# Nested 2x2 products for LSTM steps over two and three nodes, with the weight sums made in the graph stage and kept in DRAM

## The chip, the cores and the metric

The kernel runs on one core of one Trainium2 chip. Its time is the device time of one execution, in microseconds, and the median of several runs is given. The profile is of one such execution, taken by the hardware profiler.

## The reference, cut to what matters

Four layers work on `x` of 128 graphs, 64 nodes each, 256 features. The first layer, which holds all that changes, is a pre-norm residual block around two graph convolutions and four LSTMs:

```python
h = relu(layernorm(x))
h = relu(einsum('ts,bsh->bth', adj, h @ Wg0 + bg0))
h = relu(einsum('ts,bsh->bth', adj, h @ Wg1 + bg1))
for p in range(1, 5):                      # windows of p nodes
    nw = 64 // p
    wins = h[:, :nw * p].reshape(128 * nw, p, 256)
    last = lstm_last(Wih[p-1], Whh[p-1], bih[p-1], bhh[p-1], wins)   # p steps, state from zero
    h = h.at[:, arange(nw) * p + p - 1].set(last)
x = x + h

def step(h, c, x_t):                       # gates of 256 each, order i, f, g, o
    i, f, g, o = split(x_t @ Wih.T + h @ Whh.T + bih + bhh)
    c = sigmoid(f) * c + sigmoid(i) * tanh(g)
    h = sigmoid(o) * tanh(c)
```

Everything is float32. Three more layers follow (a batch-normalised graph network, a graph convolution with three weight matrices, an attention); the change does not touch them.

## The kernel before

All activations of the first layer lie feature-major in SBUF: `hT[g]`, four tiles of 128 partitions x 2 feature halves x 2048 tokens. Every engine's instructions are issued in an order that is written out by hand: functions are put on a list as events with a planned time (`at(t, fn, ...)`), the list is sorted, and the functions run in that order. Nothing is reordered afterwards; each engine and the DMA queue of SP work through their instructions in this order and wait where data or a buffer is not there.

**Graph stage** (`graph_part`, 16 rounds of 512 tokens, planned at 10 units a round). SP loads x (`load`, three buffers `xt`), DVE makes the layer norm's statistics (L375, L376, L380), POOL the root (L381), DVE the shift (L384), ACT normalises (L388). TensorE applies the adjacency (L396), the first weights (L406) and the second weights (L435); ACT copies products from PSUM (L400), DVE adds biases (L412, L442, L449). The second weights are applied in a 2x2 product form with seven products instead of eight, for which POOL makes four differences of the data a round (`sums`, L427: the tile `t`). In one of the rounds POOL also makes the four weight sums of the one-node LSTM (`weight_sum`, L313).

**The seven-product form.** A product of a 2x2 block matrix of weights with a 2x2 block matrix of data takes seven block products when four sums of weight blocks (S1 to S4) and four sums of data blocks are at hand. For one gate of an LSTM the weight blocks are the halves of its 256 inputs and 256 outputs, and the data blocks are the two feature halves of two blocks of windows (up to 512 columns each). `gate` issues these products: L701 for the input part and, in steps after the first, L707 for the state part, into the same three PSUM banks `a`, `b`, `c`. DVE and ACT take the banks to a gate tile (L723 adds, L726 copies), ACT applies the sigmoid or tanh (L719), POOL or DVE makes the new cell (L755), ACT its tanh (L760), DVE the new state (L670, L675). `input_sums` (L662) makes the four data differences of the input on DVE into `tx`, `state_sums` (L682 to L685) those of the state. There are five gate tiles and eight banks.

A first step has three gates (the state is zero, f is not needed): 21 products of 512 columns. A later step of the one-level form has four gates, each with seven input and seven state products: 56.

**The nested form** (`outer_step`), used before only for later steps over four nodes. The outer level is again a 2x2 seven-product form: the weight blocks are (input, state) x (gates i and g, gates o and f), the data blocks are x and h of the two window blocks. Of its seven products four (numbers 5, 2, 4, 3: `strassen`, L940) are themselves done in seven half-width products for each of two gates, and three (1, 6, 7: `direct`, L965) in eight plain ones. That is 28 products, each as two halves of 256 columns, and 24 whole ones: 52. The outer data sums are T1 to T4 (L1017, L1020, L1027, L1030), each of the four inner products has four inner data sums (`inner_sum`, L925), and DVE and ACT take the banks (`take`, L952 and L954; `chained`, L974 to L979). The weight sums it needs (S1 to S4 of the outer level and the inner sums of each) are made by POOL in the four-node stage itself (`outer_sum`, L874 to L885; `outer_wih_sum`, L841), and the sums for the one-level form of two and three nodes in the stage before or in their own (`weight_sums`, L313).

Two pairs of window blocks are worked on in turn (A and B), so that one's state is finished on the other engines while TensorE does the other. Two nodes have 4 pairs of 512 columns, three nodes 4 pairs (two of 320 columns and two of 352), four nodes 2 pairs of 512; one node has 8 pairs and only first steps.

Of the kernel before, what the change touches and what calls it, by code (L numbers as in the profile page):

```python
# [14 lines left out]
P = 128  # L15
# [5 lines left out]
def kernel(ctx: ExitStack, tc: tile.TileContext, a: dict, out: bass.AP):  # L21
# [317 lines left out]

    ready = []  # L340
# [12 lines left out]
    with tc.tile_pool(name="pa", bufs=2) as pa, tc.tile_pool(name="pax", bufs=3) as pax:  # L353
# [189 lines left out]
        for s in range(NS):  # L543
            graph_part(s)
        for _, _, fn, args in sorted(events, key=lambda e: e[:2]):
            fn(*args)
# [87 lines left out]
    PLACES = ("c", "a0", "b", "k0", "k1", "a1", "k2", "k3")  # L634
    new_banks(**{n: 1 for n in PLACES})
    turn_ = {"bank": 6, "gate": 0, "a": 0}

    def next_bank():
        turn_["bank"] += 1
        return bank(("c", "a0", "k0", "k1", "a1", "b", "k2", "k3")[(turn_["bank"] - 1) % 8])  # L640

    def gate_tile(k):
        return lg.tile([P, 2, KC, 512], F32, tag=f"gate{k}", name="gate")

    tx = lg.tile([P, 4, 512], F32, tag="tx", name="tx")
    lh1 = lstm.enter_context(tc.tile_pool(name="lh1", bufs=1, reuse_waits="tile"))
    even_state = ExitStack()
    lh0 = even_state.enter_context(tc.tile_pool(name="lh0", bufs=1, reuse_waits="tile"))
    events = []
# [3 lines left out]

    def input_sums(st, j):

        b = [[cols(blk, c, st["p"], j) for c in range(KC)] for blk in st["blk"]]
        t = st["tx"] = [wide(ready[0][:, n, :]) for n in range(2)] if ready else []
        ready.clear()
        yield from t
        for k in range(len(t), 4):  # L660
            t.append(wide(tx[:, k, : st["N"]]))
            yield nc.vector.tensor_sub(t[k], *((b[1][0], b[0][0]), (b[1][1], t[0]),  # L662
                                               (b[1][1], b[1][0]), (b[0][1], t[1 % len(t)]))[k])

    def state(st, n, h_of_o, last, j):

        o, tanh_c = (r["G"] for r in h_of_o)
        if last:
            for c in range(KC):
                nc.vector.tensor_mul(cols(st["blk"][n], c, st["p"], j),  # L670
                                     wide(o[:, n, c, : st["N"]]), wide(tanh_c[:, n, c, : st["N"]]))
            return
        if n == 0:
            st["h"] = st["pool"].tile([P, 2, KC, 512], F32, tag="h", name="h")
        nc.vector.tensor_mul(st["h"][:, n, :, : st["N"]], o[:, n, :, : st["N"]],  # L675
                             tanh_c[:, n, :, : st["N"]])

    def state_sums(st, engine):
        N = st["N"]
        t = st["th"] = (lh0 if st["pool"] is lh0 else sums_of).tile([P, 3, 512], F32, tag="th", name="th")  # L680
        h = st["h"][:, :, :, :N]
        yield engine.tensor_sub(t[:, 0, :N], h[:, 1, 0], h[:, 0, 0])  # L682
        yield engine.tensor_sub(t[:, 1, :N], h[:, 1, 1], t[:, 0, :N])
        yield engine.tensor_sub(h[:, 1, 0], h[:, 1, 1], h[:, 1, 0])
        yield engine.tensor_sub(t[:, 2, :N], h[:, 0, 1], t[:, 1, :N])  # L685

    def gate(t0, st, j, l, w, gi, fn):

        N = st["N"]
        blk, r = st["blk"], {"tag": turn_["gate"] % 5}  # L690
        turn_["gate"] += 1
        wih, whh = w

        def product(bank_, k):
            if bank_ not in r:
                r[bank_] = next_bank()
            first_ = (bank_, k) in (("a", 1), ("b", 5), ("c", 2))
            p_, tx = r[bank_], st["tx"]
            x_ = (cols(blk[0], 0, st["p"], j), cols(blk[0], 1, st["p"], j),
                  cols(blk[1], 1, st["p"], j), *(tx[i] if i < len(tx) else None for i in (3, 0, 1, 2)))[k - 1]  # L700
            nc.tensor.matmul(wide(p_[:, :N]), wih_of(l, k, gi), x_,  # L701
                             start=first_, stop=(j == 0), skip_group_check=True)
            if j:
                h, th = st["h"], st["th"]
                h_ = (h[:, 0, 0, :N], h[:, 0, 1, :N], h[:, 1, 1, :N], th[:, 2, :N], th[:, 0, :N],
                      th[:, 1, :N], h[:, 1, 0, :N])[k - 1]
                nc.tensor.matmul(p_[:, :N], whh[0][:, OF[k], gi, :], h_,  # L707
                                 start=False, stop=True, skip_group_check=True)

        def slot(n, hc):  # L710
            return r["G"][:, n, hc, :N]

        def new():
            r["G"] = gate_tile(r["tag"])

        def act(n, hc, bank_=None):
            m = gi * KC + hc
            to = r["G"][:, :, hc, :N] if n is None else slot(n, hc)
# [9 lines left out]
        at(t0 - 0.01, new)  # L728
# [14 lines left out]
    def wih_of(l, k, gi):  # L743
        w = wt[l][0][0]
        if l < NL - 1:
            return w[:, OF[k], gi, :]
        g, m = ORDER.index(gi), OF[k]
        if m < 4 and k != 7:
            return outer["wx"][:, m, g, :]
        return outer["wxs"][:, (S1, S2, S3, S4).index(m), g, :]  # L750

    def both(fn, st, *tiles):

        def one(n):
            fn(*((t["G"] if isinstance(t, dict) and "G" in t else st["c"])[:, n, :, : st["N"]]  # L755
                 for t in tiles))
        return one

    def tanh_of(o_, c):
        nc.scalar.activation(o_, c, AF.Tanh)  # L760

    def step(t0, st, j, last, l, w, short_next):
        p = st["p"]
        u = 1 / 1.72 if j else 1 / 0.86
        sums = input_sums(st, j)
        for k in (-0.7, 0.1, 6.3, 7.1):
            at(t0 + k, next, sums)
        g, end, t = {}, {}, t0
# [1162 lines left out]
```

## Time and profile before

| | us |
|---|---|
| median of three runs | 1864.84 (1864.15 to 1866.7) |
| the profiled execution | 1864.71 |
| its span, first to last instruction | 1863.0 |
| granted TensorE clock, mean | 0.997 |
| graph stage | 0 to 172 |
| LSTM over one node | 172 to 316 |
| over two nodes | 316 to 582 |
| over three nodes | 582 to 887 |
| over four nodes | 887 to 1206 |
| the other three layers | 1206 to 1863 |

A row of the windows gives, for a stretch of the span: its length, then for each engine its busy time with the number of instructions (PE is the matmuls, PEld the weight loads that overlap them), the granted clock, the mean share of the DMA engines and GB/s. A row of a timeline gives start, length, engine, line, operation, the tiles written and read, the shape, the count of merged instructions, and in brackets the idle time before it with what ended it. One float32 product of the program is two matmul records. Matmuls overlap in the pipeline, so the cost of one in a stream is the distance of starts and not its own length.

### The profile page before, as it was taken

Reading aid. Unit: us, or ns where it says so; the run is one execution under the profiler, and the core shown is the slowest. Engines: PE = TensorE matmul, PEld = TensorE weight load, DVE = VectorE, ACT = ScalarE, POOL = GpSimd, SP = SyncE. Lnnn points to the kernel's source line nnn. Section 1 sums busy time; section 2 is a strip of 40 time slices with the busy share of each in tenths; the row PEclk is TensorE's granted clock in tenths of the full one; section 3 lists DMA queues with packets and bytes.
Section 4 is the critical chain, followed back from the end, with each engine's and each line's share of the span. In section 5 each row is a group of like instructions: output and inputs, shape, how many; then the busy total and the mean of one; then the engine's idle time right before and its main releaser. Section 6 shows DMA issues by size and latency. Waiting matters only on the chain.

```text
span 1863.0 us, 22263 instructions
## 1 busy us (share of the span) xinstructions
PE 1832.1 (98%) x7956; PEld 1234.1 (66%) x7956; DVE 1162.3 (62%) x2250; ACT 964.1 (52%) x1680; POOL 949.1 (51%) x895
## 2 busy tenths in 40 slices
PE   8999999999999999999999999989999999999999
PEld 7997444444445666666466666656544899999997
DVE  6775777634546434444766666688876666666664
ACT  6776666534535334533534444577675454444442
POOL 4441423443423523422787776767454566666663
PEclk9999999999999999999999999999999999999999
DMA  4110000000001000000000000333110101111111
GB/s 136 57 58 0 0 1 23 23 1 0 1 0 46 1 0 1 1 1 1 23 1 1 1 1 0 102 124 114 54 40 1 46 13 46 46 46 46 46 47 35
DMA packets 51694, 55.01 MB, mean 30 GB/s; under 512 B 3456, under 2 KB 46976, under 8 KB 51584
## 3 DMA queue, kind: packets, MB, share of 16 engines
q1 hardware_dynamic: 51136, 53.30, 9.0%
q8 instruction: 63, 1.03, 0.2%
q14 instruction: 47, 0.39, 0.1%
q10 hardware_dynamic: 448, 0.30, 0.1%
HBM read 36.55 MB, written 17.04 MB: 29 GB/s over the span
## 4 chain that ended last, share of the span: by engine, by line
PE 92%; POOL 2%; DVE 2%; ACT 2%; issue 1%; DMA 1%; SPq 0%; POOLq 0%; DVEq 0%; ACTq 0%
PE ps L701 26%; PE ps L707 12%; PE ps L1655 8%; PE ps L940 7%; PE ps L965 6%; PE ps L1265 5%; PE ps L1382 4%; PE ps L396 3%; PE ps L406 3%; PE ps L1742 3%; PE ps L1622 2%; PE ps L435 2%; PE ps L1718 2%; PE ps L1752 2%; PE ps L1783 1%; PE ps L626 1%
## 5 line engine op out<-in xcount | busy, mean ns | idle before, releaser
L723 DVE TENSOR_TENSOR gate<-gate,ps 128x512 f32<-128x512 f32 (+2 forms) x306 | 176.6, 604 | 303.1 <-PE ps L707 227.6
L701 PE MATMUL ps<-tx,wih 128*128 128x512 f32 (+2 forms) x804 | 344.2, 530 | 4.2 <-ACT gate L726 3.3
L701 PE MATMUL ps<-hT,wih 128*128 128x512 f32 (+2 forms) x612 | 265.9, 530 | 0.0
L701 PEld LDWEIGHTS ps<-tx,wih 128*128 128x128 f32 x804 | 152.4, 190 | 148.0 <-issue 96.9
L726 ACT COPY gate<-ps 128x512 f32<-128x512 f32 (+2 forms) x204 | 106.2, 521 | 250.3 <-PE ps L707 195.9
L719 ACT ACTIVATE gate<-gate,lbias 128x512 f32<-128x512 f32 (+2 forms) x204 | 171.7, 842 | 117.1 <-DVE gate L723 117.0
L701 PEld LDWEIGHTS ps<-hT,wih 128*128 128x128 f32 x612 | 116.6, 190 | 108.2 <-issue 70.4
L707 PE MATMUL ps<-h,whh 128*128 128x512 f32 (+2 forms) x384 | 158.6, 494 | 0.0
L755 POOL TENSOR_TENSOR cell<-gate 128x1024 f32<-128x1024 f32 (+2 forms) x34 | 74.8, 2220 | 159.2 <-ACT gate L719 159.2
L755 POOL TENSOR_TENSOR gate<-gate 128x1024 f32<-128x1024 f32 (+2 forms) x24 | 43.9, 1851 | 181.8 <-ACT gate L719 181.8
L954 DVE TENSOR_TENSOR gate<-gate,ps 128x512 f32<-128x512 f32 x120 | 82.0, 683 | 69.4 <-PE ps L940 67.0
L707 PE MATMUL ps<-th,whh 128*128 128x512 f32 (+2 forms) x288 | 118.9, 494 | 0.0
L1598 ACT ACTIVATE h<-x,ln_rn 128x256 f32<-128x256 f32 x128 | 68.0, 592 | 92.8 <-POOL ln_rn L1595 92.7
L1655 PE MATMUL ps<-wl,ag 128*128 128x128 f32 x900 | 108.3, 276 | 0.6
L707 PEld LDWEIGHTS ps<-h,whh 128*128 128x128 f32 x384 | 73.0, 190 | 54.3 <-issue 30.6
L1655 PEld LDWEIGHTS ps<-wl,ag 128*128 128x128 f32 x900 | 104.2, 192 | 3.3 <-ACT ag L1627 2.5
L985 ACT ACTIVATE gate<-gate,lbias 128x512 f32<-128x512 f32 x96 | 64.9, 717 | 57.4 <-DVE gate L954 30.3
L707 PEld LDWEIGHTS ps<-th,whh 128*128 128x128 f32 x288 | 54.7, 190 | 40.7 <-issue 23.0
L755 POOL TENSOR_TENSOR cell<-gate,cell 128x640 f32<-128x640 f32 (+2 forms) x20 | 37.2, 1874 | 67.4 <-ACT gate L719 67.4
L726 DVE COPY gate<-ps 128x512 f32<-128x512 f32 (+2 forms) x102 | 62.0, 608 | 13.0 <-PE ps L707 12.6
L1742 PE MATMUL ps<-wvo,h3T 128*128 128x256 f32 x256 | 65.5, 379 | 0.0
L760 ACT ACTIVATE gate<-cell 128x1024 f32<-128x1024 f32 (+2 forms) x60 | 55.5, 931 | 18.6 <-POOL cell L755 18.6
(317 smaller groups left out, 4098.5 us busy)
## 6 DMA issues: line engine op xcount, KB each, us to landing
xt<-in_x_dram SPq DMA_DIRECT2D x30, 512.0 KB, 3.9
x1d<-xt SPq DMA_DIRECT2D x16, 512.0 KB, 2.9
x<-x1d SPq DMA_DIRECT2D x16, 512.0 KB, 4.8
out_dram<-x SPq DMA_DIRECT2D x15, 512.0 KB, 3.0
wih<-in_WihT_dram SPq DMA_DIRECT2D x12, 256.0 KB, 4.9
whh<-in_WhhT_dram SPq DMA_DIRECT2D x8, 256.0 KB, 5.6
xt<-in_x_dram SPq DMA_DIRECT2D x6, 128.0 KB, 3.5
wl<-in_W_dram SPq DMA_DIRECT2D x4, 192.0 KB, 3.1
```

What stands on the lines that cost most here:

```text
L701: nc.tensor.matmul(wide(p_[:, :N]), wih_of(l, k, gi), x_, start=first_, stop=(j == 0), skip_group_check=True)
L707: nc.tensor.matmul(p_[:, :N], whh[0][:, OF[k], gi, :], h_, start=False, stop=True, skip_group_check=True)
L719: nc.scalar.activation(to, r[bank_][:, :N] if bank_ else to, fn, bias=lbias[:, l, m : m + 1])
L723: nc.vector.tensor_add(slot(n, hc), slot(n, hc), r[bank_][:, :N])
L726: op(slot(n, hc), r[bank_][:, :N])
L755: fn(*((t["G"] if isinstance(t, dict) and "G" in t else st["c"])[:, n, :, : st["N"]] for t in tiles))
L940: nc.tensor.matmul(B[pr, name][:, g * H : (g + 1) * H], w[:, g, :], d, start=(g == 0 and (name, k) in (("a", 1), ("b", 5), ("c", 2))), sto ...
L954: nc.vector.tensor_add(half(pr, hc, d), half(pr, hc, d), v)
L965: nc.tensor.matmul(to, w, d, start=(pr == 1 and c == 0), stop=(c == 1), skip_group_check=True)
L1265: nc.tensor.matmul(r[name], con["w1"][:, OF[j], g, :], x_, start=new, stop=(name, j) in (("a", 4), ("b", 3), ("c", 2)), skip_group_check=True)
L1655: nc.tensor.matmul(v["g", name][:, p_, :], x_[:, m, ts(p_, P)], wl2[:, OF[j], m, :], start=new and p_ == m == 0, stop=m == 2 and (name, j) ...
L1742: nc.tensor.matmul(v["H"][:, q % 2, :], v["h3T"][:, c, ts(q, P)], wvo[:, c, :], start=(c == 0), stop=(c == KC - 1))
```

## The change

All steps after the first, over two and three nodes too, use `outer_step`; `gate` keeps the first steps only, and the one-level later step goes. The weight sums of the LSTMs over two, three and four nodes are made by POOL during the graph stage (`staging`), one layer after the other in one place (`wb`, `wc`), and stored to DRAM (`summed`). The LSTM stages fetch them into places that are free at the time (`places`, `fetch`, `load_r`, `fetch_s3`); for two nodes two places overlap and are refilled in every group. The differences of the input for first steps are made by POOL instead of DVE. The order of banks and gate tiles at group starts is written out, and the inner data sums of the state are planned later in `outer_step`, because three of the inner products share one place for them. The ends of the stage (`begin` and what follows it) keep their planned times in a new unit.

```diff
+    def staging(p):
+        R = wbf[:, :2048].rearrange("p (b g m) -> p b g m", b=4, m=P)
...
+        IG, OF_ = R[:, :, 0:2], R[:, :, 2:4]
+        add, sub = nc.gpsimd.tensor_add, nc.gpsimd.tensor_sub
+        work = [*(inner(W1, k) for k in (0, 1, 3)), *(inner(W2, k) for k in (0, 1, 3)),
+                *(outer(add, S1_, OF_, W2, b) for b in (0, 2)), *(outer(sub, S2_, S1_, IG, b) for b in (0, 2)),
+                inner(W2, 2), *(inner(S1_, k) for k in range(4)),
+                *(outer(sub, S4_, W1, S2_, b) for b in (0, 2)), inner(W1, 2),
+                *(x_sum(k) for k in range(4)), *(inner(S4_, k) for k in range(4)),
+                *(outer(sub, OF_, IG, OF_, b) for b in (0, 2))]
+        stores = {9: ("S2", wbf[:, 5632:6656]), 10: ("W2", w2), 14: ("S1", wcf), 17: ("W1", w1),
+                  21: ("X", wbf[:, 5632:]), 25: ("S4", w2)}
+        loads = [lambda: load("WhhT", W1, ((0, 0), (1, 2))), lambda: load("WhhT", W2, ((0, 3), (1, 1))),
+                 lambda: load("WihT", R, tuple(enumerate(ORDER)))]
+        def last():
+            nc.sync.dma_start(summed[p, "S3"].rearrange("p (b g m) -> p b g m", b=4, m=P), OF_)
...
+        def stage(n, fn):
+            r, k = divmod(n, 6)
+            events.append((30 + ROUND * r + (-0.7, 0.5, 1.7, 2.9, 4.1, 5.3)[k], len(events), fn, ()))
+        for i, p in enumerate(range(2, NL + 1)):
+            work, stores, loads = staging(p)
+            for n, fn in enumerate(work):
+                stage(28 * i + n, fn)
+            for n, fn in stores.items():
+                stage(28 * i + n + 1, fn)
+            for n, fn, t in zip((18, 26, 28), loads, (10.5, 17.5, 24.5)):
+                if i:
+                    stage(28 * (i - 1) + n + 1, fn)
+                else:
+                    events.append((t, len(events), fn, ()))
...
-            yield nc.vector.tensor_sub(t[k], *((b[1][0], b[0][0]), (b[1][1], t[0]),
+            yield nc.gpsimd.tensor_sub(t[k], *((b[1][0], b[0][0]), (b[1][1], t[0]),
...
+    def fetch(p, name, lo=0, hi=7):
+        to = pl[p][name]
+        g = to.parts[0].shape[2]
+        v = summed[p, name].rearrange("p (b g m) -> p b g m", g=g, m=P)
+        hi = min(hi, v.shape[1])
+        cuts = sorted({lo, hi, *(c for c in to.cuts if lo < c < hi)})
+        for b0, b1 in zip(cuts, cuts[1:]):
+            nc.sync.dma_start(to.span(b0, b1), v[:, b0:b1])
...
-        for k in (-0.7, 0.1, 6.3, 7.1):
-            at(t0 + k, next, sums)
+        for k in (-9, -8.5, 0.2, 0.4) if st["new"] else (*((-0.8, -0.6) if p == NL else (-3.4, -1.4)), 2.6, 6.6):
+            at(t0 + k, next, input_)
...
         for c in range(KC):
-            prep(-38 + 0.6 * c, T1, c, needs_h=False)
+            tick((-26 if one else -38) + 0.6 * c, T1, c)
...
-        for k, s in ((0, -25), (1, -24), (3, -23)):
+        prep(-11, T2)
+        prep(-10.9, inner_sum, 5, 2)
+        for k, s in ((0, 1), (1, 2), (3, 3)):
             prep(s, inner_sum, 2, k)
...
-        for k in range(4):
-            prep(late + 2 + k, inner_sum, 4, k)
+        for k, s in ((0, 25), (1, 26), (3, 27), (2, 28)):
+            prep(s, inner_sum, 4, k)
+        for k, s in ((0, 38), (1, 38.5), (3, 39), (2, 39.5)):
+            prep(s, inner_sum, 3, k)
...
+    plan(t, 2, (2, load_r), *((8 + 3 * k, fetch, name) for k, name in enumerate(("X", "W1", "W2", "S1", "S2"))),
+         (25, fetch, "S4", 2, 7), (28, fetch_s3, 0))
     for p in range(1, NL + 1):
...
+            if p == 2:
+                plan(t, p, (8, fetch, "S4", 0, 2))
+            if p == NL:
+                plan(t, p, (8, fetch, "S4"), (8.5, fetch_s3, 0))
+            now = {"22": tags[1], "11": tags[2], "12": tags[3], "21": tags[4], "spare": tags[0]}
+            t += 1
+            for j in range(1, p):
+                for st in sts:
+                    fin = p == NL and j == p - 1 and st is sts[-1]
+                    u = t
+                    t = outer_step(t, st, j, now, fin)
+                    tags = [now[n] for n in ("spare", "11", "21", "12", "22")]
+                    now = dict(now)
+                    now["22"], now["spare"] = now["spare"], now["22"]
+            if p == 2 and not end:
+                plan(u, p, (43, fetch, "X", 2, 4))
+            if end and p < NL:
+                q = p + 1
+                plan(u, q, (12.5, load_r), (36, fetch, "X"), (25.5, fetch, "W1"), (38.5, fetch, "W2"),
+                     (52.5, fetch, "S1"), (53.5, fetch, "S2"))
+                if q < NL:
+                    plan(u, q, (68, fetch, "S4"), (70, fetch_s3, 0))
```

## The prediction

> **What bounds the kernel now.** I read the page's first part, then the windows by stage, then the PE timeline at one place of each stage, then POOL's timeline in the graph stage.
>
> ```profile
> PE 1832.1 (98%) x7956; PEld 1234.1 (66%) x7956; DVE 1162.3 (62%) x2250; ACT 964.1 (52%) x1680; POOL 949.1 (51%) x895
> ```
>
> TensorE is busy 98% of the span, so only fewer matmul columns or fewer stalls can move the time. The stages (busy us: PE, PEld, DVE, ACT, POOL):
>
> ```profile
> 0.00:172.00 172.00, 165.09 (x991) 149.89 (x992) 114.67 (x317) 116.76 (x192) 68.97 (x105) 1.00 0.23 68
> 172.00:316.00 144.00, 143.33 (x334) 63.20 (x334) 105.46 (x156) 97.61 (x134) 38.54 (x18) 1.00 0.00 0
> 316.00:582.00 266.00, 265.58 (x622) 117.80 (x621) 132.66 (x173) 115.13 (x157) 102.53 (x54) 1.00 0.03 8
> 582.00:887.00 305.00, 303.53 (x1066) 201.84 (x1065) 149.64 (x280) 134.56 (x245) 109.75 (x77) 1.00 0.03 8
> 887.00:1206.00 319.00, 312.84 (x1090) 204.14 (x1088) 209.51 (x294) 144.49 (x228) 236.93 (x173) 0.99 0.06 19
> ```
>
> They are the graph stage and the LSTMs over one, two, three and four nodes. No engine but PE is near full, except POOL in the last (74%). What a product costs, from the PE timeline of the four-node stage (already nested) and of the three-node stage:
>
> ```profile
> 946.41 1.03 PE L940 MATMUL ps<-mid,whh 128*128 128x256 f32 x4
> 947.27 1.02 PE L965 MATMUL ps<-th,mid 128*128 128x512 f32 x2
> 948.13 1.03 PE L940 MATMUL ps<-h,whh 128*128 128x256 f32 x4
> ```
> ```profile
> 641.45 0.70 PE L707 MATMUL ps<-th,whh 128*128 128x320 f32 x2
> 641.99 0.76 PE L701 MATMUL ps<-hT,wih 128*128 128x352 f32 x2
> 642.58 0.76 PE L707 MATMUL ps<-h,whh 128*128 128x352 f32 x2
> ```
>
> A product is two records. Starts give 0.86 us for 512 columns, 0.86 for its two halves of 256, 0.54 for 320 and 0.59 for 352.
>
> Stalls, from the PE timeline around the start of the four-node stage:
>
> ```profile
> 906.86 1.88 PE L701 MATMUL ps<-hT,wih 128*128 128x512 f32 x4
> 911.00 2.80 PE L701 MATMUL ps<-tx,wih 128*128 128x512 f32 x4 [2.26 <-ACT gate L726]
> 913.60 1.91 PE L701 MATMUL ps<-hT,wih 128*128 128x512 f32 x2
> 915.30 1.06 PE L701 MATMUL ps<-tx,wih 128*128 128x512 f32 x2
> ...
> 936.18 2.07 PE L965 MATMUL ps<-hT,wih 128*128 128x512 f32 x2 [2.54 <-ACT gate L719]
> ```
> ```profile
> 911.00:940.00 29.00, 26.46 (x67) 13.86 (x68) 18.87 (x20) 13.31 (x20) 28.61 (x22) 0.88 0.00 1
> ```
>
> The 2.26 us gap is followed by products at 1.70 us instead of 0.86 (913.60 to 915.30), and the granted clock is 0.88 in that window. By starts the two stalls cost 4.2 and 4.3 us. POOL is busy 28.61 of 29 us there.
>
> **The change part by part.**
>
> *Products.* An LSTM step after the first takes 2 x 28 = 56 products now and 4 x 7 + 3 x 8 = 52 nested, 28 of them as two halves. Two nodes (512 columns): 4 pairs x 1 step x 4 products x 0.86 = 13.8 us less; the halves add 28 x 0.003 a step (4 x 216 ns against 2 x 429), so 13.4. Three nodes: 4 steps at 320 columns, 4 x 4 x 0.54 = 8.6, and 4 at 352, 4 x 4 x 0.59 = 9.4. Halves of 160 and 176 columns are in no row; 128-column matmuls of L1655 start 112 ns apart, 256-column ones 216. A straight line between them gives 138 and 151 ns, half of the full width plus 1.5 ns gives 136 and 149. So 15.1 to 17.0 us. The sum is 28.5 to 30.3; I take **-29.5**.
>
> [...] The rows above decide: the halves cost 0.86 against 0.86, at 128 columns weight loads still keep up with 112 ns, and 160 lies between. I use the rows.
>
> *Weight sums, moved into the graph stage.* Off POOL in the LSTM stages go L313's wih and whh sums of two and three nodes (8 x 1.34 + 8 x 1.44), L841 (3.9) and L874 to L885 (some 27): about 53 us, 27 of them inside the window at 911. Into the graph stage come 84 sums in 14 rounds of six: 48 of 256 columns (0.70 us from start to start), 24 of 512 (1.25), 12 of 384 (1.0), 76 us, or 5.4 a round. A round:
>
> ```profile
> 88.76 0.73 POOL L427 TENSOR_TENSOR t<-g 128x256 f32<-128x256 f32 x1 [4.97 <-ACT g L400]
> ...
> 92.30 1.01 POOL L381 TENSOR_TENSOR ln_rn<-ln_rn,mhalf 128x4 f32<-128x4 f32 x1
> 93.28 5.10 POOL L313 TENSOR_TENSOR wih<-wih 128x512 f32<-128x512 f32 x4
> 98.81 0.73 POOL L427 TENSOR_TENSOR t<-g 128x256 f32<-128x256 f32 x1 [0.43 <-ACT g L400]
> ```
>
> A round is 10.05 us, four differences and the root take 3.8, so 6.25 are free: 5.4 fits. But the round at 93.3 already holds the 5.1 us of the one-node weights; with its own 5.3 the differences end some 4 us late. PE first reads t at 104.65 and today has 5.1 us of slack, so that alone just fits; the root, 4 us late, holds DVE's L384 (due at 104.62, slack 1.3), behind it ACT's relus and g copy (L400 ends at 107.43, PE needs it at 109.49). Cost: 4 - 1.3 - 2.1 = 0.7 us.
>
> *SP's queue.* Moved ahead of the x loads: 48 weight loads (0.65 us each to issue) and 21 stores, each store behind its POOL sum, and a load into the same place behind the store's landing. At the turn from two to three nodes: S4's sum ends at 74.6, its 0.9 MB store lands about 4 us later (estimate from x1d's 2.9 us for 0.5 MB), four loads to 81.2, S3's store, eight loads to 87, and only then the x load that today goes out at 67.6. It lands at 90.5; DVE's statistics want it at 87.5. DVE stands 3 us, with evictions queued behind it; PE has 2.75 us there. But the root is now late by as much and POOL waits in it, just ahead of the overfull round: t is ready at 106.9 against 104.65, PE stands 2.3 us, then some 1 us for root and relus. The later x loads that follow stores and weight loads come out some 3 us late at worst, which those 2.75 us cover.
>
> [...] The row at 911.00 shows half speed after 2.26 us. [...] by the row some 1.6 us more; I use the row. Graph stage: 0.7 without the late x load, 5 with it, 9 if DVE's stands reach PE too. I take **+4**.
>
> *DMAs in the LSTM stages.* 54 fetches, loads and refills, all behind PE's last read of the place and 6 to 40 us ahead of first use; after the x loads nothing else waits in SP's queue. 0, hidden behind PE's steps; a late one would cost its landing, 3 to 6 us.
>
> *Input differences on POOL.* One-node stage: DVE loses four L662 a step (0.68 to 1.1 us), POOL gains four. L682, 512 columns on POOL, takes 1.27 us. POOL has then 5.1 + 2 x 2.4 = 9.9 of 18 us a step. The tightest is the fourth: it follows both cell products and ends 1.2 us ahead of its reader. 0; if POOL runs as in its contended rows (2.7 for 2.4), up to 0.5 a step, 8 steps, 4 us.
>
> *Other engines in nested steps.* At 320 columns: POOL 8 operations of 640 (1.55) and 16 of 160 (0.53, by the line through 455 ns at 128 and 730 at 256), 21 of 28 us; DVE 32 x 0.48 plus six SBUF operations, 21; ACT 12 x 0.42 + 16 x 0.56 + 1.5 = 16. All below PE. At four nodes the same mix runs with no gap.
>
> *Stalls at group starts.* Now, in starts: 0.7 at 458, 0.4 and 0.9 at 589 and 613, 1.5 at 737, 4.2 and 4.3 at the four-node start: 12 us. After, five groups enter the nested form. Their first steps load ACT with 2 x 10 us plus the tail of the step before (7) in 24 us at three nodes, so some queueing stays: I give each group 1.6 us, as at 737, 8 in all. **-4**. Bounds: -11 (none left) to +10.
>
> Sum: -29.5 + 4 - 4 = -29.5. Against the profiled execution of 1864.71 (span 1863.0 and 1.7 around it; the median of the three runs, 1864.84, is 0.1 above): **1835**.
>
> **The rivals.** *R1, the graph stage hardly notices and nested entries are clean*: for it, POOL's free 6.25 against 5.4 and the gapless four-node steps; against, the overfull round. -29.5 - 10 + 1: 1826. *R2, POOL bounds the graph stage*: if its sums run at contended durations (L925 at 1.04 us for 256, L885 at 1.6 for 512), a round has 7.5 against 6.25, 14 x 1.25 = 17 us, with 4 from the x load: 1852. Against it: in this stage L427 and L313 run uncontended. *R3, slower*: entering the nested form costs what it costs today at the only place where it is entered, 8.5 us. Four more groups enter it: +34 - 29.5, and the graph stage's 4: 1873. It decides from 6.4 us an entry ((29.5 - 4) / 4). Against it: at 911 to 940 POOL was full of weight sums that are gone, and DVE stood behind it:
>
> ```profile
> 900.80 2.68 DVE L662 TENSOR_TENSOR tx<-hT,tx 128x512 f32<-128x512 f32 x1
> ```
>
> *R4, the change does not do what it says* is excluded as to products: the program has 52 of them a step.
>
> **How the numbers follow.** My forecast 0.62 (1835, its bounds 1829 to 1843), R1 0.18, R2 0.14, R3 0.06. The range 1825 to 1847 takes in R1, mine and R2's nearer half. About 0.2% (3.7 us) is what a measurement of this kernel can tell from no change. Faster 0.94, same 0.01, slower 0.05.
>
> **What would show it.** Products: 128x160 and 128x176 records some 136 to 151 ns apart; two- and three-node stages of some 253 and 289 us. Graph stage: POOL near 95%, a PE gap near 105, an x wait of DVE near 87.5, the stage longer by 1 to 9 us. Four-node start: no gap above 2 us. Wrong if halves start over 165 ns apart, if DVE or POOL end waits within the nested steps, or if each group start shows gaps above 3 us.

## The result, and the profile after

| | before | after |
|---|---|---|
| median of four runs each, us | 1864.49 (1862.59 to 1866.70) | 1838.02 (1836.51 to 1839.84) |
| ratio | | 0.9858, 95% interval 0.9841 to 0.9875 |
| the profiled execution, its span | 1864.71, 1863.0 | 1838.82, 1837.1 |
| first LSTM product starts at | 171.8 | 178.7 |
| from it to the last nested product of the four-node stage | 1033.1 | 1000.1 |
| from there to the end | 658.0 | 658.3 |

The change is worth 26.5 us. The LSTM stages lose 33.1 us, the graph stage gains 6.9, the rest is as it was. The last three rows are read off TensorE's starts in the two traces, and are used for every run below.

The first part of the page after, to be read against the line of before that the prediction shows:

```profile
PE 1802.4 (98%) x8532; PEld 1299.3 (71%) x8532; DVE 1196.0 (65%) x2346; ACT 990.8 (54%) x1776; POOL 1211.8 (66%) x1207
```

TensorE still bounds the kernel with 98%, on a shorter span. POOL, 949 us before, has 1212: the staged sums and the input differences.

The windows by stage (graph stage to the first LSTM product; to the first nested product; to the first three-node product; to the first four-node product; to the last nested one). The columns are busy us of PE, PEld, DVE, ACT and POOL, then granted clock, DMA share, GB/s; the length of the stretch stands ahead of them:

```profile
0.00:178.70 178.70, 166.69 (x990) 149.60 (x991) 119.83 (x317) 117.15 (x192) 144.09 (x189) 1.00 0.57 188
178.70:357.31 178.61, 177.94 (x415) 78.62 (x414) 97.65 (x156) 119.90 (x167) 96.45 (x63) 1.00 0.09 33
357.31:575.18 217.87, 217.87 (x732) 138.61 (x730) 133.31 (x184) 100.49 (x153) 140.95 (x104) 1.00 0.09 28
575.18:866.12 290.94, 286.65 (x1450) 231.59 (x1449) 195.89 (x369) 150.70 (x308) 212.50 (x217) 1.00 0.07 23
866.12:1178.76 312.64, 310.50 (x1090) 202.98 (x1089) 199.21 (x290) 145.96 (x231) 224.42 (x168) 1.00 0.06 19
```

Most of TensorE's idle time sits in two rows: 12.0 us in the graph stage (6.9 in the shorter window of before) and 4.3 us in the three-node stage; the four-node stage has 2.1 us. The nested two-node steps have none.

The PE timeline within a three-node step of 352 columns, nested now:

```profile
782.42 0.76 PE L985 MATMUL ps<-hT,wc 128*128 128x352 f32 x2
783.01 0.76 PE L961 MATMUL ps<-h,wb 128*128 128x176 f32 x4
783.61 0.76 PE L985 MATMUL ps<-hT,wc 128*128 128x352 f32 x2
784.20 0.76 PE L961 MATMUL ps<-h,wb 128*128 128x176 f32 x4
```

Four half-width records take 0.60 us (783.01 to 783.61), two whole ones 0.59. By the median of all starts a record of 176 columns takes 149 ns, of 160 columns 136, of 256 columns 216; whole ones of 352, 320 and 512 take 296, 269 and 429.

The graph stage, on TensorE, POOL and DVE:

```profile
97.55 0.67 PE L493 MATMUL ps<-t,wg 128*128 128x256 f32 x2 [2.30 <-DVE h L507]
111.57 0.70 PE L493 MATMUL ps<-g,wg 128*128 128x256 f32 x2 [1.86 <-DVE h L500]
143.02 0.70 PE L493 MATMUL ps<-g,wg 128*128 128x256 f32 x2 [0.94 <-DVE h L500]
```
```profile
89.86 2.54 POOL L370 TENSOR_TENSOR wc<-wb 128x512 f32<-128x512 f32 x2 [2.79 <-DMA wb<-in_WihT_dram]
...
109.39 1.02 POOL L439 TENSOR_TENSOR ln_rn<-ln_rn,mhalf 128x4 f32<-128x4 f32 x1
...
137.29 0.73 POOL L313 TENSOR_TENSOR wb<-wb 128x256 f32<-128x256 f32 x1 [3.47 <-issue]
```
```profile
92.03 0.43 DVE L433 BATCH_NORM_STATS2 ln_st<-xt 128x6 f32<-128x256 f32 x1 [4.19 <-DMA xt<-in_x_dram]
110.45 0.68 DVE L442 SCALAR_TENSOR_TENSOR ln_rn<-ln_mv,ln_rn 128x4 f32<-128x4 f32 x1 [2.94 <-POOL ln_rn L439]
```

Three gaps of TensorE, all released by DVE. DVE was late for x (due near 87.8, there at 92.00) and twice for POOL's root: L439 ends at 110.4, and before the third gap DVE stood another 1.68 us for it, at 141.89. POOL itself stood twice for a weight load of the staging: for R at 89.86, and at 137.29, where the profile names no releaser ("issue") but the last load of the four-node W2 (the third W2) had landed at 137.17.

The largest gaps that are left in the LSTM stages, three-node and four-node starts:

```profile
588.74 1.40 PE L853 MATMUL ps<-tx,wih 128*128 128x320 f32 x4 [1.70 <-ACT gate L869]
...
674.36 0.78 PE L961 MATMUL ps<-h,wb 128*128 128x160 f32 x4 [0.63 <-POOL wb L947]
...
892.89 1.12 PE L853 MATMUL ps<-tx,wb 128*128 128x512 f32 x2 [0.53 <-ACT gate L869]
894.28 1.13 PE L853 MATMUL ps<-tx,wb 128*128 128x512 f32 x2 [0.27 <-POOL tx L818]
```

The four-node start, which stood 2.26 and 2.54 us before and ran at half speed after each (granted clock 0.50 for 3.41 us from 911.97 and from 935.86), has no gap above 0.6.

### The profile page after: what moved, and what is told of

It is laid out like the page before. It is cut to its first block, busy times and chain, and to the rows that moved or that the text cites. A ratio compares the mean times of both kernels' runs of the same rounds, so it can differ in the third digit from the quotient of the medians.

```text
span 1837.1 us, 24418 instructions
## 1 busy us (share of the span) xinstructions
PE 1802.4 (98%) x8532; PEld 1299.3 (71%) x8532; DVE 1196.0 (65%) x2346; ACT 990.8 (54%) x1776; POOL 1211.8 (66%) x1207
## 4 chain that ended last, share of the span: by engine, by line
PE 89%; POOL 5%; ACT 2%; issue 2%; DVE 1%; DMA 1%; SPq 0%; POOLq 0%; DVEq 0%; ACTq 0%
PE ps L961 20%; PE ps L985 16%; PE ps L853 14%; PE ps L1672 8%; PE ps L1282 5%; PE ps L1399 4%; PE ps L1759 3%; PE ps L1639 3%; PE ps L454 2%; PE ps L1735 2%; PE ps L464 2%; PE ps L493 2%; PE ps L1769 2%; PE ps L1800 1%; PE ps L700 1%
## 5 line engine op out<-in xcount | busy, mean ns | idle before, releaser
L972 DVE TENSOR_TENSOR gate<-gate,ps 128x512 f32<-128x512 f32 (+2 forms) x360 | 216.7, 603 | 171.9 <-PE ps L961 160.1
L1005 ACT ACTIVATE gate<-gate,lbias 128x512 f32<-128x512 f32 (+2 forms) x288 | 175.7, 653 | 166.9 <-DVE gate L972 84.2
L866 DVE TENSOR_TENSOR gate<-gate,ps 128x512 f32<-128x512 f32 (+2 forms) x162 | 100.7, 640 | 128.7 <-PE ps L853 118.7
L853 PE MATMUL ps<-tx,wih 128*128 128x512 f32 (+2 forms) x276 | 117.9, 544 | 3.0 <-ACT gate L869 2.5
L1015 POOL TENSOR_TENSOR gate<-gate 128x1024 f32<-128x1024 f32 (+3 forms) x37 | 73.5, 1986 | 63.1 <-ACT gate L1005 63.1
L862 ACT ACTIVATE gate<-gate,lbias 128x512 f32<-128x512 f32 (+2 forms) x108 | 95.7, 886 | 29.0 <-DVE gate L866 28.9
L999 DVE TENSOR_TENSOR gate<-gate,ps 128x512 f32<-128x512 f32 (+2 forms) x144 | 80.7, 602 | 21.6 <-PE ps L985 19.6
L961 PE MATMUL ps<-h,wb 128*128 128x256 f32 (+2 forms) x392 | 91.5, 356 | 1.9 <-POOL wb L947 1.3
L853 PEld LDWEIGHTS ps<-tx,wih 128*128 128x128 f32 x276 | 51.5, 190 | 57.1 <-issue 39.7
L985 PE MATMUL ps<-hT,wb 128*128 128x512 f32 x160 | 81.7, 592 | 0.0
L900 POOL TENSOR_TENSOR cell<-gate 128x1024 f32<-128x1024 f32 (+2 forms) x36 | 78.1, 2191 | 5.4 <-ACT gate L862 5.4
L985 PE MATMUL ps<-wih,thA 128*128 128x512 f32 (+2 forms) x192 | 79.3, 495 | 0.0
L853 PE MATMUL ps<-hT,wih 128*128 128x512 f32 (+2 forms) x168 | 78.4, 571 | 0.0
L1021 POOL TENSOR_TENSOR cell<-cell,gate 128x1024 f32<-128x1024 f32 (+3 forms) x37 | 75.5, 2041 | 2.9
```

Of the source, the lines that this page charges most:

```text
L853: nc.tensor.matmul(wide(p_[:, :N]), wih_of(p, k, gi), x_, start=first_, stop=True, skip_group_check=True)
L862: nc.scalar.activation(to, r[bank_][:, :N] if bank_ else to, fn, bias=lbias[:, l, m : m + 1])
L866: nc.vector.tensor_add(slot(n, hc), slot(n, hc), r[bank_][:, :N])
L900: nc.gpsimd.tensor_mul(cell[:, n, :, :N], i, g_)
L961: nc.tensor.matmul(B[pr, name][:, g * H : (g + 1) * H], w[:, g, :], d, start=(new and g == 0), stop=(name, k) in (("a", 4), ("b", 3), ("c" ...
L972: nc.vector.tensor_add(to, to, v)
```

## The experiments

Each median is of four or five executions, timed beside the kernel before (medians of before: 1863.90 for the next four rows below "after", 1864.28 for thin sums and the two with the late tanh, 1864.71 for the rest). "Graph" is the start of the first LSTM product, "LSTM" the time from it to the last nested product; these two are read from one traced execution of each kernel.

| kernel | median, us (range) | ratio to before, 95% | graph | LSTM |
|---|---|---|---|---|
| before | 1864.49 | | 171.8 | 1033.1 |
| after | 1838.02 (1836.51 to 1839.84) | 0.9841 to 0.9875 | 178.7 | 1000.1 |
| one-node sums late | 1836.09 (1834.86 to 1836.19) | 0.9833 to 0.9863 | 174.7 | 1000.1 |
| x early | 1838.24 (1836.18 to 1840.07) | 0.9842 to 0.9875 | 179.1 | 1000.0 |
| both | 1833.54 (1833.01 to 1833.82) | 0.9821 to 0.9850 | 173.6 | 1000.1 |
| x early, sums where POOL stood | 1834.97 (1832.39 to 1836.18) | 0.9827 to 0.9856 | 174.3 | 1000.0 |
| empty places ahead of R | 1832.89 (1832.61 to 1833.87) | 0.9818 to 0.9845 | 172.4 | 1000.6 |
| thin sums | 1835.14 (1834.12 to 1836.09) | 0.9829 to 0.9856 | 175.1 | 1000.1 |
| differences on DVE | 1846.84 (1844.37 to 1849.11) | 0.9890 to 0.9921 | 177.6 | 1008.4 |
| POOL filled at the four-node start | 1850.64 (1849.41 to 1852.68) | 0.9915 to 0.9940 | 178.3 | 1013.4 |
| both of these | 1851.87 (1851.12 to 1852.78) | 0.9921 to 0.9946 | 177.5 | 1015.7 |
| late tanh | 1843.76 (1841.69 to 1844.60) | 0.9874 to 0.9901 | 179.0 | 1007.2 |
| late tanh and empty places | 1838.95 (1837.12 to 1842.78) | 0.9850 to 0.9882 | 171.8 | 1007.7 |

### Where the graph stage's 6.9 us come from

My theory was the one of the prediction: a round in which POOL has too much, and an x load behind stores and weight loads. The rival was POOL's own standing for weight loads.

**One-node sums late.**

```diff
-    at(1.4 + 1.3 * k, lambda k=k: weight_sum(wih0[0], k))
+    at(75.5 + 0.1 * k, lambda k=k: weight_sum(wih0[0], k))
```

> The changed kernel with one edit: the four sums of the one-node weights (POOL, 5.1 us) go from the round at about 104 us to the end of the graph stage, behind the last staged sum. Theory A (the round with both loads is overfull, and its late root makes the 1.86 us gap of TensorE at 111.6): that gap is gone, the first LSTM product comes 2 us earlier (178.7 to about 176.7), time about 1836. The 2.30 us gap at 97.5 and the 0.94 us gap at 143.0 stay. Theory B (POOL is late at 111 because it stood 2.79 us for the loaded R at 89.86, and never recovers): the gap at 111.6 stays at 1 us or more, time within 0.5 us of 1838. Third outcome, a cost: the sums now end near 178, beside the first one-node products; if they are late there, a gap of 1 to 3 us appears at 174 to 182.

In the traces the first LSTM product comes 4.0 us earlier, not 2. The medians differ by 1.9 us: the traced execution, 1834.86, is the fastest of its four, and the others, at 1836.06 to 1836.19, have no trace. The PE timeline where the gap at 111.6 was:

```profile
108.38 1.05 PE L454 MATMUL ps<-adjT_bd,ln_h 128*128 128x128 f32 x8
109.28 0.60 PE L493 MATMUL ps<-g,wg 128*128 128x256 f32 x2
109.71 0.59 PE L493 MATMUL ps<-t,wg 128*128 128x256 f32 x2
```

Product follows product. The gap at 143.0 has gone as well, which I had expected to stay: POOL had carried its lateness 30 us on. The root L439 ends at 106.2 here, 4.2 us earlier. POOL's stand for R (3.13 us) and the gap at 97.6 (2.65 us) are still there, so theory B is wrong for the gap at 111.6.

**x early.**

```diff
-            at(-21, load)
+            at(-31 if s >= 5 else -21, load)
```

> The changed kernel with one edit: from the sixth round on the x load stands ten units (about 10 us) earlier in SP's order. Theory A (the load of x behind two stores and twelve weight loads makes DVE stand 4.19 us at 92.03 and TensorE 2.30 us at 97.5): DVE's wait and that gap are gone; what follows of lateness at 111.6 (1.86 us) shrinks but does not go, since the round is overfull; first LSTM product 2.5 to 4 us earlier, time 1834.5 to 1836. Theory B (POOL's own standing for the weight loads, 2.79 us at 89.86 and 3.47 us at 137.29, holds the root, and DVE would stand for the root instead of x): the gap at 97.5 stays above 1 us, time above 1837. A cost: x then shares the DMA engines with the stores, POOL's stands for weights grow by up to 2 us each.

Theory B. DVE no longer stands for x, and nothing is won: the first LSTM product is 0.4 us later. The same place on TensorE, POOL and DVE:

```profile
97.95 0.70 PE L493 MATMUL ps<-g,wg 128*128 128x256 f32 x2 [1.29 <-DVE h L500]
111.40 0.70 PE L493 MATMUL ps<-g,wg 128*128 128x256 f32 x2 [1.86 <-DVE h L500]
```
```profile
89.85 2.55 POOL L370 TENSOR_TENSOR wc<-wb 128x512 f32<-128x512 f32 x2 [2.66 <-DMA wb<-in_WihT_dram]
...
95.22 1.02 POOL L439 TENSOR_TENSOR ln_rn<-ln_rn,mhalf 128x4 f32<-128x4 f32 x1
```
```profile
96.28 1.22 DVE L442 SCALAR_TENSOR_TENSOR ln_rn<-ln_mv,ln_rn 128x4 f32<-128x4 f32 x1 [1.50 <-POOL ln_rn L439]
```

POOL works in order, so its stand for R holds the differences and the root behind it; DVE now stands for that root instead of x. The two waits lie side by side, and taking one away leaves most of the other. The gap at 97.5 shrinks by 1.0 us and that at 143 grows from 0.94 to 1.45; a new one of 0.39 us at 107.1 has POOL's t as its releaser.

**Both.**

> The changed kernel with both edits: one-node weight sums at the end of the graph stage and the x load ten units earlier. If the two causes are separate and are all there is: gaps at 97.5 and 111.6 gone, the 0.94 us at 143.0 left, first LSTM product at about 173.3 to 174.5, time 1832.5 to 1834. If POOL's stands for its weight loads are the third cause: the gap at 143 stays or grows, first product near 175 to 176, time 1834.5 to 1836.

173.6 and 1833.54, as named for two separate causes, but not with the gaps named: the one at 143 is gone, and one is left behind R. The parts do not add, they open each other. Alone they bring 4.0 and -0.4, together 5.1 (by the medians 1.9, -0.2 and 4.5). The gap that is left:

```profile
97.42 0.70 PE L493 MATMUL ps<-g,wg 128*128 128x256 f32 x2 [1.11 <-DVE h L500]
```

**x early, and the sums where POOL stood.**

```diff
-    at(1.4 + 1.3 * k, lambda k=k: weight_sum(wih0[0], k))
+    at((-6.2, -6.1, 35.1, 35.2)[k], lambda k=k: weight_sum(wih0[0], k))
```

> The changed kernel with the x load ten units earlier, and the one-node weight sums put where POOL stands today: two of them (2.6 us) ahead of the first sum that needs R (POOL idle 2.79 us at 89.86), two ahead of the first that needs the third W2 (idle 3.47 us at 137.29). Theory: POOL's stands shrink to below 1 us each, and nothing is added to POOL, so first product at 172.5 to 174, time 1832 to 1833.5, below the one with the sums at the end by 0 to 1.5 us; the 0.94 us gap at 143.0 stays, for the root is as late as before. Rival: POOL's standing moves with its sums (it still stands for the DMA, the sums only delay it): time as with x early alone, 1834.5 to 1836.

POOL's stand for R falls to 0.39 us as the theory said, but the root is no earlier (DVE's L442 waits 1.81 us for it) and the gap at 98.0 is 1.61 us. The time, 1834.97, is the rival's, though the stand did shrink. Filling a wait is free only when nothing stands behind it; the first product comes at 174.3, later than with the sums at the end.

**Empty places ahead of R.** The root and the differences of the round go ahead of the sum that waits for the DMA:

```diff
-        def stage(n, fn):
+        def stage(n, fn, d=0):
+            n += 2 * (n >= 34) + (n >= 59) + d
             r, k = divmod(n, 6)
...
```

(`d` keeps each store or load one place behind its sum), together with the x load ten units earlier and the one-node sums among the last staged ones (`at(70.6 + 0.1 * k, ...)`).

> The changed kernel with the x load ten units earlier, the one-node sums among the last staged sums, and the staged sums from the first that needs R on two places later in POOL's order, from the second standing on three: the root and the differences of that round are then ahead of the sum that waits for the DMA. Theory (POOL, in order, standing for a weight load, holds the root behind it; that is the 1.11 us gap that stays at 97.4 with both earlier edits): the gap at 97.4 is gone, no gap of TensorE above 0.5 us between 85 and 170, first LSTM product at 172.3 to 173 (with the two earlier edits 173.6, in the kernel before 171.8), time 1832 to 1833. Rival: the gap at 97.4 comes from DVE, late by its own queue; it stays, time 1833.5.

The POOL timeline shows the order that was wanted, without a wait for a DMA:

```profile
92.90 1.01 POOL L439 TENSOR_TENSOR ln_rn<-ln_rn,mhalf 128x4 f32<-128x4 f32 x1
93.88 2.54 POOL L370 TENSOR_TENSOR wc<-wb 128x512 f32<-128x512 f32 x2
```

The root ends at 93.9 instead of 96.4, and from 85 to 165 there is no gap of TensorE at all. From TensorE's first product of the program (at 7.1 here, 6.5 before) to the first LSTM product it is 165.3 us, as in the kernel before: the staged sums cost the graph stage nothing in this order. At 1832.9 this has the lowest median, 5.1 us below the change as it was made; its range overlaps that of "both", so it is the gap that is gone, not the time, that tells the theory from the rival. Its LSTM part gave 0.5 us back: the last staged sum ends at 177.6, and POOL's first input differences stand behind it, for which TensorE waits at 178.9.

**Thin sums.** The 84 staged sums are cut to 8 of the 128 columns of each block; the rest of them is not computed, and every load and store stays. `to[:, bs]` becomes `to[:, bs, :, :8]`, and so on.

> The changed kernel with its 84 staged sums cut to 8 of the 128 columns of each block (the rest of each sum is not computed; places read without being written are set to zero once at the start), and every load and store of the staging as it was. It parts POOL's time in the graph stage (76 us) from the DMAs in SP's queue. If the x load behind the stores and weight loads is what costs (the step of the forecast): the 2.30 us gap at 97.5 stays, the others go, first LSTM product at 174 to 175. If POOL's time costs: first product at 172 to 172.5 and no gap at 97.5, for with short sums the stores and loads go out earlier too. POOL's stand for R at 89.86 may stay or grow, since the sums that filled the time are short; if it holds the root, DVE's L442 shows it.

Setting places to zero at the start delayed TensorE's first product by 2.5 us (9.2 against 6.7), so 175.1 reads as 172.6. DVE's stand for x (2.98 us) and POOL's for R (2.98) are still there, the gap at 98.0 is 0.66 us, and no other in the graph stage is above 0.3. So nearly all of the 6.9 us is POOL's time. The late x cost 0.7 us here, where POOL had room to catch up; counted from TensorE's first product it came 1.6 us earlier than in the change, so this is a lower bound.

### What cleared the four-node start

**Differences on DVE**, weight sums staged as in the change:

```diff
-            yield nc.gpsimd.tensor_sub(t[k], ...
+            yield nc.vector.tensor_sub(t[k], ...
```

> The changed kernel with one edit: the input differences of the first LSTM steps back on DVE, the weight sums staged as in the changed kernel. Theory A (the place of the differences is worth nothing by itself; what cleared the four-node start is that POOL no longer makes weight sums there): the four-node start keeps gaps below 1 us, and the gaps of TensorE released by POOL's differences (0.32 us at 577.3, 0.27 at 894.3) go; time 1836.5 to 1838.5. Theory B (moving the differences off DVE is what cleared it): gaps of 1.5 us or more return near 893 and 918, a lowered clock with them, time 1841 to 1847.

Neither theory in its place, B in size: the LSTM stages are 8.3 us longer (8.8 by the medians of the whole), but at group starts of two, three and four nodes, and at full clock there (two records of 512 columns behind the gap take 1.13 us, in after at 892.89 1.12). The PE timelines around 472, 595, 741 and 895:

```profile
472.50 1.13 PE L853 MATMUL ps<-tx,wb 128*128 128x512 f32 x2 [1.53 <-DVE gate L866]
...
595.42 0.81 PE L853 MATMUL ps<-tx,wih 128*128 128x320 f32 x2 [1.67 <-DVE gate L866]
...
740.74 0.81 PE L853 MATMUL ps<-tx,wih 128*128 128x320 f32 x2 [1.33 <-DVE gate L866]
...
895.39 1.13 PE L853 MATMUL ps<-tx,wb 128*128 128x512 f32 x2 [2.16 <-DVE gate L866]
```

DVE's adds out of the banks stand behind the differences, and those behind the states of the step before. On DVE, and on POOL, ahead of 595:

```profile
591.13 0.51 DVE L818 TENSOR_TENSOR tx<-hT,tx 128x352 f32<-128x352 f32 x1
591.57 1.62 DVE L1030 TENSOR_TENSOR hT<-gate 128x512 f32<-128x512 f32 x2
593.11 1.85 DVE L818 TENSOR_TENSOR tx<-hT 128x352 f32<-128x352 f32 x1
594.88 0.91 DVE L866 TENSOR_TENSOR gate<-gate,ps 128x320 f32<-128x320 f32 x2
```
```profile
592.57 3.80 POOL L900 TENSOR_TENSOR cell<-gate 128x640 f32<-128x640 f32 x2 [0.53 <-ACT gate L862]
```

The difference at 593.11 takes 1.85 us against 0.51 for the one of its shape at 591.13, and TensorE gets its bank only from the add behind it. The long one ran beside POOL's product of the cells (L900). That is so at all four places: the last difference ahead of the add takes 1.85 to 2.83 us, 1.3 to 2.2 us more than without a POOL operation beside it, which is about the gap of TensorE. So more than the order counts here; no run parts the two.

**POOL filled at the four-node start**, with 27 us of unused subtractions:

```diff
+            if p == NL and k == 0:
+                v = thA[:, 1024:1536]
+                for d in range(21):
+                    at(t + 13.05 + 2 * d, nc.gpsimd.tensor_sub, v, v, v)
```

> The changed kernel with one addition: 21 subtractions of 512 columns on POOL, in place, on a part of a tile that nothing reads any more (they compute nothing that is used), two units apart from the middle of the first four-node step on: some 27 us of POOL's time at the place where the kernel before made its weight sums. Theory A (POOL crowded with sums held the cell products and through them ACT and TensorE: 2.26 and 2.54 us at 911 and 936 before): gaps of 1.5 us and more come back between 885 and 925, in all 4 to 9 us, time 1842 to 1847. Theory B (the stall came from DVE's input differences behind POOL, or from the order of the steps, both changed now): gaps below 1 us each, time within 2 us of 1838.

Theory A, and dearer than expected: 13.3 us. The PE timeline at the start of the four-node stage:

```profile
895.08 1.12 PE L853 MATMUL ps<-tx,wb 128*128 128x512 f32 x2 [1.60 <-ACT gate L869]
899.56 2.08 PE L853 MATMUL ps<-tx,wb 128*128 128x512 f32 x2 [3.35 <-POOL tx L818]
901.42 3.62 PE L853 MATMUL ps<-hT,wb 128*128 128x512 f32 x4
904.84 0.99 PE L853 MATMUL ps<-tx,wb 128*128 128x512 f32 x1
...
929.70 2.05 PE L961 MATMUL ps<-wc,wb 128*128 128x256 f32 x4 [2.80 <-DVE gate L972]
```

Four records of 512 columns in 3.4 us (901.42 to 904.84) instead of 1.72: half speed again (granted clock 0.84 over 885 to 905). The worst gap waits for the fourth input difference, which is on POOL now and stands behind the filling.

**Both of these.**

> The changed kernel with both: the input differences on DVE and the 27 us of unused subtractions on POOL at the four-node start. If POOL's load alone makes the stall, as with the load alone (within 1 us of it). If it takes both, as the kernel before had both: the load alone costs below 2 us, this costs 6 to 9 us, time 1844 to 1847. If neither does, because the order of the steps made it: within 2 us of 1838.

15.7 us more than after in the LSTM stages, of which one to three nodes have 6.2, about as with the differences on DVE alone, and the four-node stage 9.5. There the load alone costs 13.3, the differences on DVE alone 2.2. So POOL's load makes the stall by itself, and the whole is 1.2 us above the load alone. In the four-node stage the differences are better off on DVE with POOL filled, and better off on POOL with POOL free: there the two halves of the change need each other.

### A try at the gaps that are left

**Late tanh.**

```diff
-        tick(e + (6.5 if last and p < NL else 4.2), squash, 1)
-        tick(e + (8.8 if last and p < NL else 6), out, 1)
+        tick(e + (10.5 if last and p < NL else 4.2), squash, 1)
+        tick(e + (11.8 if last and p < NL else 6), out, 1)
```

> The changed kernel with one edit: the last tanh of a group's cells (ACT L1024), and the product behind it on DVE, stand four and three units later, behind the next group's two copies out of the banks. Theory A (ACT, in order, stands 2.85 us for POOL's L1021 at 586.87, and the copies that empty TensorE's banks stand behind it): the 1.70 us gap at 588.7 goes, LSTM stages 1.5 to 2.5 us shorter (1000.1 to about 998), time about 1836. Theory B (ACT and DVE are simply full there, two first steps and the tail of the step before in 24 us): the gap moves to the next copy, at 590 to 597, and the stages stay within 0.5 us of 1000.1. A cost: the states come out 2 us later, and POOL's differences of the next group with them; gaps of POOL's tx of 0.5 us and more.

A miss for both theories. ACT's copies come in time and the gap at 588.7 is gone, but now DVE stands for the tanh, with the adds out of the banks behind it:

```profile
595.56 2.33 DVE L1030 TENSOR_TENSOR hT<-gate 128x512 f32<-128x512 f32 x2 [2.26 <-ACT gate L1024]
597.82 0.90 DVE L866 TENSOR_TENSOR gate<-gate,ps 128x320 f32<-128x320 f32 x2
```

At 473.7 the add costs a gap of 3.01 us and a stretch of half speed (two records of 512 columns from 473.69 to 475.43, 1.74 us instead of 0.86). The LSTM stages are 7.2 us longer.

**Late tanh with the empty places.**

> Everything that pointed downwards at once: x load ten units earlier, one-node sums among the last staged sums, the empty places in POOL's order ahead of R and the third W2, and the last tanh of a group behind the next group's copies. If the parts add: first LSTM product at 172.4, LSTM stages as in the kernel with the late tanh alone (998 if its gap goes), time 1830.5 to 1831.5 against 1832.9 without the late tanh. If the late tanh brings nothing: 1832.5 to 1833.3.

The graph stage is as short as hoped (171.8), and the late tanh costs what it cost alone: 1838.95 against 1832.89 without it. The gaps of 0.8 us (start to start) at 674 and 818, where POOL's inner sums come late, and the one at 588.7 stay open; no run here removed them with a gain.

## Why the prediction was right, and where its steps were not

The time, 1838.0, lies 3 us above the forecast of 1835. By terms:

| step | forecast, us | measured, us |
|---|---|---|
| products | -29.5 | -30.1 |
| graph stage | +4 | +6.9 |
| stalls at group starts | -4 | -3.0 |
| input differences on POOL | 0 | inside the line above; 8.3 if taken back |
| DMAs in the LSTM stages | 0 | no gap of TensorE there is released by a DMA |

The measured line of the stalls sums, over the LSTM stages, what TensorE's starts lie further apart than the usual pitch of their shape, without some 2 us at the end of the four-node stage that both kernels have: 13.0 us before, 9.9 after. The products are what is left of the 33.1 us, and pitch by pitch they give the same 30.1: 13.1 for two nodes, 8.0 and 9.0 for three.

*Products.* Right. Halves of 160 and 176 columns start 136 and 149 ns apart, the lower end of what I gave. The rows of before, which I followed, were right, now also at these widths. The working has a slip: four halves of 216 ns are 6 ns more than two wholes of 429, not 3, so two nodes win 13.1 us and not 13.4. The one-node stage is 145.1 us in both kernels; two nodes, from 323.84 on, take 251.3 us and three 290.9, against 253 and 289 named. Neighbouring stages overlap, so the sum tells more: 542.3 against 542.

*Graph stage.* The kind was right: DVE's stand for x (I said near 87.5, landing at 90.5; it was due at 87.8 and landed at 92.0), the overfull round, the late root. I named one gap near 105; there were three, at 97.6, 111.6 and 143.0. POOL is busy for 81% of the stage (144.09 of 178.70 us), not near 95. The term that was mis-sized is the overfull round, 0.7 us: taking it away brought 4.0 in the traces and 1.9 by the medians. I had counted a single round's lateness against that round's slack. What I left out is that POOL has only 0.85 us of spare time in a round, so lateness from one round is still there three rounds later, and that POOL itself stands for R and W2, 2.79 and 3.47 us, with the root and the differences behind. I had followed SP's queue as far as x and not as far as POOL's own reads of those loads. The x load, for which I took 2.3 us and more, decides little: early alone it brings nothing, on top of the late sums 1.1 us (2.6 by the medians).

*The clock.* I added 1.6 us for half speed after a gap of some 2.3 us, by the row at 911.00. In the profile of after the 2.30 us gap is followed by products at full pace (granted clock 1.00 over 97 to 103 us), so the 1.6 us were not there. That was luck: in three other runs the same place lost the clock (0.72 over the same 6 us), after 2.04 us ("both of these"), 2.49 ("differences on DVE") and 2.82 ("late tanh"); see the last section.

*Stalls.* That the sum of -4 was near is luck, for its parts were not. The four-node start fell from 8.6 to 1.7 us, more than I gave it; the stalls of the two- and three-node stages rose from 3.5 to 7.3. I had counted the move of the differences as nothing, because DVE and POOL had room on average. With DVE the LSTM stages are 8.3 us longer: at a group start the two-level tail of the step before and two first steps meet, and there an engine's order decides, and how long its operations last beside another's (one difference of 352 columns took 0.51 us, the next of that shape, beside POOL's product, 1.85), not its average.

*Rivals.* R1 (clean, 1826) fails on both its terms. R2 named the right engine for the wrong reason: POOL's sums ran at 0.7 us for 256 columns, not at 1.04; what made it late was one overfull round and two waits. R3 (each nested entry costs 8.5 us) fell as argued: without weight sums on POOL the four-node entry costs 1.7. Filling POOL brought the stall back, so the reason given against R3 is shown.

## What to carry to other kernels

Work moved to an engine that has free time costs nothing only if it is never ahead, in that engine's order, of something that a busier engine waits for; look at every wait that the moved work itself brings, and put it behind the urgent operations of its round: here the staged sums cost the graph stage 6.9 us in one order and nothing in another. Two late inputs that lie side by side hide each other: taking away one can show nothing, and only the pair shows what it was worth. Where several engines are 60 to 70% busy (here DVE 65%, POOL 66%), the ends and beginnings of groups decide, and one operation's engine or place there can be worth much: here 8.3 us for the differences, more than a quarter of what the fewer products bring.

## What the runs showed of the hardware that was not expected

Idles of TensorE of about one length were followed by full pace in one run and by half speed in another. The same place of the graph stage, in two runs: the PE timelines of "one-node sums late" and of "differences on DVE", which have the same instructions there on TensorE, then the windows behind the gap in the same order (PE's busy time is the second number, the granted clock the third from the end):

```profile
97.61 0.67 PE L493 MATMUL ps<-t,wg 128*128 128x256 f32 x2 [2.65 <-DVE h L507]
98.11 1.05 PE L454 MATMUL ps<-adjT_bd,ln_h 128*128 128x128 f32 x8
...
99.87 1.05 PE L454 MATMUL ps<-adjT_bd,h 128*128 128x128 f32 x8
```
```profile
97.96 0.86 PE L493 MATMUL ps<-t,wg 128*128 128x256 f32 x2 [2.49 <-DVE h L507]
98.61 1.91 PE L454 MATMUL ps<-adjT_bd,ln_h 128*128 128x128 f32 x8
...
101.88 1.05 PE L454 MATMUL ps<-adjT_bd,h 128*128 128x128 f32 x8
```
```profile
98.00:102.00 4.00, 4.00 (x33) 3.87 (x32) 2.73 (x9) 3.34 (x7) 3.92 (x6) 1.00 0.56 221
```
```profile
98.00:102.00 4.00, 4.00 (x16) 3.58 (x17) 1.35 (x4) 2.71 (x6) 4.00 (x5) 0.57 0.32 131
```

After 2.65 us of idle eight records take 0.9 us, after 2.49 us of idle 1.7 us. From the first product behind the gap to the adjacency's second group (99.87 and 101.88) it is 2.26 us in one run and 3.92 in the other, 1.66 us more. It is 3.92 us in "late tanh" too, behind 2.82 us of idle. In "both of these", behind 2.04 us, half speed comes later in the group: up to the product that follows it (L209) it is 4.81 us there and 3.15 in "one-node sums late", again 1.66 us more. The idles of 2.26 and 2.54 us at the four-node start of before lost the clock, the one of 2.30 at 97.5 in after did not. So of these seven idles of 2.04 to 2.82 us five were followed by half speed, and the two that were not, 2.30 and 2.65 us, lie between them: the length alone did not tell which. What did is not shown by these runs.

Every stretch of half speed of the traces of before and after, between start and end of the program, is 3.41 us long: at 911.97, 935.86 and 1219.17 before, at 1192.79 after. The last of before and the one of after come with an idle behind the LSTM stages, of 3.16 and 3.07 us.

The granted clock differs between executions of one kernel as well. Of the nine executions of before that were timed beside "empty places ahead of R", six had a mean granted clock of 0.997 and took 1864.59 to 1866.76 us, three had 0.999 and took 1861.28 to 1863.30.

DVE's differences of two SBUF tiles lasted longer beside POOL. In "differences on DVE" those of 512 columns take 0.68 to 0.69 us in all 32 cases without a POOL operation beside them, and up to 2.83 us in the 22 with one; in before (L662, 512 columns) it is 0.68 to 0.69 us in 46 cases without and 0.68 to 2.85 us in 24 with. The add out of a bank (L866, 512 columns; L723 in before) takes 0.67 to 0.69 us in all 126 cases of "differences on DVE" and all 174 of before, with POOL beside it or not.
